# Sums of weights beside bank reads: fw2's first sums in pieces of 256 columns, three of fw1's sums one stage sooner, ScalarE first in block 1's products

## The chip, the cores and the metric

The kernel runs on one core of a Trainium2 chip. A core has five engines with a queue each: TensorE (PE in the profile; its weight loads are the row PEld), VectorE (DVE), ScalarE (ACT), GpSimd (POOL) and SyncE (SP, which here only issues DMAs). Each engine works through its queue in the order in which it was written, and waits on semaphores of the others. The metric is device time in microseconds for one launch, the median of several runs.

## The reference

One transformer-like block on x of 2 x 2048 tokens by 512 features, all in fp32, with six modulation rows from a condition:

```python
emb = silu(t) @ ada_w + ada_b
shift_msa, scale_msa, gate_msa, shift_mlp, scale_mlp, gate_mlp = split(emb, 6)
norm = ln(x) * (1 + scale_msa) + shift_msa
h = gelu(norm @ ssm_w1 + ssm_b1)                  # 512 -> 512
x = x + gate_msa * (h @ ssm_w2 + ssm_b2)          # 512 -> 512
norm2 = ln(x) * (1 + scale_mlp) + shift_mlp
hf = gelu_tanh(norm2 @ ff_w1 + ff_b1)             # 512 -> 1024
x = x + gate_mlp * (hf @ ff_w2 + ff_b2)           # 1024 -> 512
```

## The kernel before

The 4096 tokens are eight blocks of 512, four per batch element. Each block passes four products: hA (with w1), oA (with w2), hC (with fw1) and oC (with fw2). They are staggered: while PE works on hC and oC of block i, the other engines prepare the normalized and transposed input (nT) of later blocks.

To save matmuls, every product of two matrices is done in quarters by a scheme of seven products in place of eight (P1 to P7, Strassen-Winograd). Its price is sums of quarters on both sides. Four sums are needed for a side: two of them go in place or into a new tile first, the other two follow. `sums_of_first` and `sums_of_second` write them, and `cut_sum` (L311) issues them, whole or in pieces along the second axis. Sums of weights are done once (fw2's again for the second batch element), sums of activations (nS, hSA, hSC) for every block. PE's own order of the seven is P1, P2, P6, P5, P7, P3, P4. They accumulate in PSUM banks with the tags y, x, y, v, y, v, y, so a bank must be read out before a later product adds to it. `group` (L391) issues them; after each one a reader on DVE or ACT takes the bank. For hA and hC these are L565 or L563 (first use), L571, L578 and L581 on DVE and activations on ACT (L572, L579, L582, L585), for oA and oC L613 on DVE.

Block 0's hC is done so, in two groups. From block 1 on hC is one list of 26 products (`products`, L712), of sums of 4 x 4 quarters of fw1 with sums of 4 x 2 quarters of the activations, which stand in place of 32. For this fw1's 16 quarters and 12 further places are turned into 28 registers by 37 sums (`HK_A`, in pieces of 256 columns, L650, or L648 where the sum is negated), all on DVE. They are taken off a list in order: `take(n)` gives the next n to the hooks of a stage. The activations' side (`HK_B`, 20 sums, L650) runs on POOL. A product's bank is read into one or two of eight destinations: a destination's first read is a copy with a sign on ACT (L726), later ones are adds on DVE (L729). Where one bank has readers of both kinds, they are ordered: the second waits for the first.

```python
for turn in (fresh_reads, other_reads)[:: 1 if last else -1]:
```

decides which goes first; `last` is true for block 7 only.

Nothing is scheduled automatically: each engine's order is the order in which the program is written. Helpers take `hooks`, lists of small operations that are called after a given product, and so land at that place in their engine's queue.

Around the change the stages are, by PE's time in the profile: oA_1 (to 72 us), hC_0 group 0 (to 85), hC_0 group 1 (85 to 98.6), hA_2 (98.6 to 110.7), oC_0 (110.7 to 134.9), block 1's products (134.9 to 159.3), oA_2. In hC_0 group 1 POOL has, at P6, fw2's first two sums (`fold5(8, 10)`), then the sums of nT of block 2 (nS, L311), fw2's third sum, and the sums of hC's output (hSC). fw2's fourth sum and the 20 sums of `HK_B` follow in hA_2 and oC_0. In the same stages DVE has the sums of fw1: two in hC_0 group 1, eight and then four at the end in hA_2, eighteen in oC_0, the last five in the products. It also reads the banks, turns nT of block 1 (L476) and takes statistics (L425, L426) of block 3. fw1's upper right part is loaded again (L933, 512 KB) in hC_0 group 1, since the first scheme's sums have overwritten it.

Of the kernel before, what the change touches and what calls it, by code (L numbers as in the profile page):

```python
# [38 lines left out]
ALU = mybir.AluOpType  # L39
# [101 lines left out]
def kernel(  # L141
# [16 lines left out]
    nc = tc.nc  # L158
# [148 lines left out]
    def cut_sum(eng, out, a, b, f, cut):  # L307

        n = out.shape[1] // cut
        for r in [slice(c * n, (c + 1) * n) for c in range(cut)]:  # L310
            eng.tensor_tensor(out[:, r], a[:, r], b[:, r], f)  # L311
# [7 lines left out]
            lambda: cut_sum(eng, s[2], q["12"], s[0], ALU.subtract, cut),  # L319
        ]  # L320

    def sums_of_second(q, s, eng, last_cut=1):

        return [
            lambda: cut_sum(eng, s[1], q["22"], q["12"], ALU.subtract, 1),
            lambda: cut_sum(eng, q["12"], q["12"], q["11"], ALU.subtract, 1),
            lambda: cut_sum(eng, s[0], q["22"], q["12"], ALU.subtract, last_cut),
            lambda: cut_sum(eng, s[2], q["21"], s[0], ALU.subtract, last_cut),
        ]

    def first_operands(q, s):
# [2 lines left out]
    def second_operands(q, s):  # L334
        return {"P1": q["11"], "P2": q["21"], "P3": q["22"], "P4": s[2], "P5": q["12"], "P6": s[0], "P7": s[1]}

    def thirds(t):
        return [t[:, j] for j in range(3)]
# [12 lines left out]
        for n, w in (("w2", w2), ("fw2", fw2))  # L351
    ]

    def weight_of_second(w_sb, s, gt, engs, last_cut=1):

        K = w_sb.shape[1]

        def fold(k):
            engs[k % len(engs)].tensor_tensor(w_sb[:, k, :], w_sb[:, k, :], gt, ALU.mult)

        ops = [lambda k=k: fold(k) for k in range(K)]
        lo, hi = w_sb[:, : K // 2, :], w_sb[:, K // 2 :, :]
        q = {
            "11": lo[:, :, : D // 2],
            "12": lo[:, :, D // 2 :],
            "21": hi[:, :, : D // 2],
            "22": hi[:, :, D // 2 :],
        }
        s = thirds(s)
        return second_operands(q, s), ops + sums_of_second(q, s, nc.gpsimd, last_cut)  # L370

    Q = P // C
    ORDER = ("P1", "P2", "P6", "P5", "P7", "P3", "P4")
# [32 lines left out]
    def hook(hooks, places, ops):  # L406

        for n, op in enumerate(ops):
            hooks.setdefault(places[min(n, len(places) - 1)], []).append(op)


    class Norm:
# [117 lines left out]
        def summed(self, eng):  # L530

            s = thirds(sums.tile([P, 3, C, KD // 2, HT // C], F32, tag="s", name=f"nS{self.name}"))
            h = self.nT.rearrange("p a (k h r) -> p a k h r", k=KD, h=2)
            lo, hi = h[:, :, : KD // 2], h[:, :, KD // 2 :]
            q = {
                "11": lo[:, :, :, 0],
                "12": lo[:, :, :, 1],
                "21": hi[:, :, :, 0],
                "22": hi[:, :, :, 1],
            }  # L540
            self.ops = second_operands(q, s)
            return sums_of_second(q, s, eng)
# [99 lines left out]
    def sums_of_registers(program, reg, engs):  # L642


        def op(n, d, f, a, b):
            eng = engs[n % len(engs)]
            if f == "n":
                nc.vector.scalar_tensor_tensor(reg[d], reg[a], -1.0, reg[b], ALU.mult, ALU.subtract)  # L648
            else:
                eng.tensor_tensor(reg[d], reg[a], reg[b], ALU.add if f == "+" else ALU.subtract)  # L650

        return [lambda z=(n,) + step: op(*z) for n, step in enumerate(program)]
# [19 lines left out]
    class Second:  # L672
# [6 lines left out]
        def group(self, g, rhs, hooks):  # L679
            hidden(f"hC_{self.i}_{g}", rhs, fw1_ops, fb1T, AF.Gelu_apprx_tanh, self.lo, self.hi, g, hooks)  # L680

        def products(self, fa, fb, hooks, last=False):


            ends = {b: n for n, (b, *_) in enumerate(HK_P)}
            starts = [(n, b) for n, (b, fresh, *_) in enumerate(HK_P) if fresh]
            stops = set(ends.values())
            for n, b in starts:
                stops |= {max([m for m in range(n) if HK_P[m][0] == b], default=ends[b])}
            ps = {  # L690
                b: ps_g.tile([P, 2, HT], F32, tag=tag, name=f"p{tag}_hC_{self.i}_{b}")
                for b, tag in HK_BANK.items()
            }
            left = [sum(d == r for (*_, rs) in HK_P for r, _ in rs) for d in range(8)]
            fresh_dest, done = set(range(8)), []

            def dest(d):
                f, col = d // 2, d % 2
                h = (self.lo, self.hi)[f // 2]
                return h[:, 2 * (f % 2) : 2 * (f % 2) + 2, col * HT : (col + 1) * HT]  # L700

            def activate():
                for d in done:
                    for j in range(2):
                        h = dest(d)[:, j]
                        m = 2 * (d // 2) + j
                        nc.scalar.activation(h, h, AF.Gelu_apprx_tanh, bias=fb1T[:, m : m + 1])  # L707
                done.clear()

            for n, (b, fresh, ra, rb, reads) in enumerate(HK_P):  # L710
                for j in range(2):
                    nc.tensor.matmul(  # L712
                        ps[b][:, j, :],
                        fa[ra][:, j * P : (j + 1) * P],
                        fb[rb].rearrange("p a (c q) -> p c a q", q=Q),
                        start=(fresh and j == 0),
                        stop=(n in stops),
                        skip_group_check=True,
                    )
                fresh_reads = [r for r in reads if r[0] in fresh_dest]  # L720
                other_reads = [r for r in reads if r not in fresh_reads]
                fresh_dest -= {d for d, _ in fresh_reads}
                for turn in (fresh_reads, other_reads)[:: 1 if last else -1]:
                    for d, sign in turn:
                        if turn is fresh_reads:
                            nc.scalar.activation(dest(d), ps[b], AF.Identity, scale=float(sign))  # L726
                        else:
                            op = ALU.add if sign > 0 else ALU.subtract
                            nc.vector.tensor_tensor(dest(d), dest(d), ps[b], op)  # L729
                activate()  # L730
                for d, _ in reads:
                    left[d] -= 1
                    if not left[d]:
                        done.append(d)
                for op in hooks.get(n, ()):
                    op()
            activate()
# [87 lines left out]
    def ssm_gate():  # L825
        make_gate(2, 0)
        found["w2"] = weight_of_second(w2_sb, w2_s, gate[2, 0], (nc.vector,))
# [7 lines left out]
    hooks = {}  # L835
# [12 lines left out]
    hooks = {}  # L848
# [12 lines left out]
    def ff_gate():  # L861
        make_gate(5, 0)
        found["fw2"] = weight_of_second(fw2_sb, fw2_s, gate[5, 0], (nc.vector,), 4)

    def fold5(lo, hi):
        return [lambda k=k: found["fw2"][1][k]() for k in range(lo, hi)]

    def gb5_0():
# [5 lines left out]
    hooks = {}  # L874
# [20 lines left out]
    hooks = {}  # L895
# [13 lines left out]
    hC = Second(0)  # L909
    n2[1] = Norm(1, 2)  # L910
    hooks = {}
# [8 lines left out]
    fa = [fw1_sb[:, k, f * 2 * P : (f + 1) * 2 * P] for f in range(4) for k in range(KD)] + [  # L920
        fw1_s[:, s, k, c * 2 * P : (c + 1) * 2 * P] for s in range(3) for k in range(2) for c in range(2)
    ]
    fb, fa_sums = {}, sums_of_registers(HK_A, fa, (nc.vector,))

    def take(n):
        ops = fa_sums[:n]
        del fa_sums[:n]
        return ops
# [8 lines left out]
    hooks = {}  # L937
# [10 lines left out]
    hooks = {}  # L948
    hook(hooks, ("P1",), hC.summed(1, nc.gpsimd, 2))
    hook(hooks, ("P4",), n2[1].moved() + fold5(11, 12))  # L950
    hook(hooks, ("P1", "P2", "P6", "P6", "P5", "P5", "P7", "P3"), take(8))
    hA[2] = First(2, n1[2].ops, hooks, on_act=True)
    run(take(4))
    n1[3] = Norm(3, 1)
    hooks = {}
# [11 lines left out]
    for i in range(1, NBLK):  # L967
        nxt, nx2, last = i + 1 < NBLK, i + 2 < NBLK, i + 1 == NBLK
        hC = Second(i)
        hooks = {}  # L970
# [11 lines left out]
        if fold:  # L982
            hook(hooks, (2, 6, 23, 25), fold[:4])
        hook(hooks, (20,), hC.summed(0, nc.gpsimd))
        hC.products(fa, fb[i], hooks, last)

        hooks = {}
        hook(hooks, EARLY, hC.summed(1, nc.gpsimd if nxt else nc.vector))
# [15 lines left out]
        hooks = {}  # L1004
# [54 lines left out]
        if refold5:  # L1059
            load_w("fw2", fw2, fw2_sb)  # L1060
            make_gate(5, b)
            fw2_ops, fold = weight_of_second(fw2_sb, fw2_s, gate[5, b], (nc.vector,))
        hooks = {}
# [52 lines left out]
```

## Time and profile before

| | us |
|---|---|
| median of 3 runs | 603.66 |
| lowest, highest | 603.02, 604.52 |
| the profiled execution | 603.54 |
| its span, first to last instruction | 601.7 |
| PE busy in the span | 592.5 (98%) |
| DVE, ACT, POOL busy | 376.1, 218.7, 397.1 |
| granted TensorE clock | 0.999 |

The profile shows one execution. A row of a timeline gives the start, the duration, the engine, the line, the operation, what it writes and reads, the tile's size and the count, and in brackets how long the engine was idle before it and what released it. A row of the waits view gives the engine and tile that waited, the one waited for, the total in us, how often, and the longest. Busy time of PE is modelled from its instructions, so starts are the better measure.

### The profile page before, as it was taken

Reading aid. Unit: us, or ns where it says so; the run is one execution under the profiler, and the core shown is the slowest. Engines: PE = TensorE matmul, PEld = TensorE weight load, DVE = VectorE, ACT = ScalarE, POOL = GpSimd, SP = SyncE. Lnnn points to the kernel's source line nnn. Section 1 sums busy time; section 2 is a strip of 40 time slices with the busy share of each in tenths; the row PEclk is TensorE's granted clock in tenths of the full one; section 3 lists DMA queues with packets and bytes.
Section 4 is the critical chain, followed back from the end, with each engine's and each line's share of the span. In section 5 each row is a group of like instructions: output and inputs, shape, how many; then the busy total and the mean of one; then the engine's idle time right before and its main releaser. Section 6 shows DMA issues by size and latency. Waiting matters only on the chain.

```text
span 601.7 us, 8144 instructions
## 1 busy us (share of the span) xinstructions
PE 592.5 (98%) x2827; PEld 509.8 (85%) x2827; DVE 376.1 (63%) x638; ACT 218.7 (36%) x363; POOL 397.1 (66%) x459
## 2 busy tenths in 40 slices
PE   8999999999999999999999999999999999999997
PEld 4787887887888888888888888888888888888886
DVE  5978988997754475645754458644565336467642
ACT  3234247304532254323731346123553225212420
POOL 2878688998735896549978398885983695540110
PEclk9999999999999999999999999999999999999999
DMA  8980222300223003340051611321020300022001
GB/s 323 413 349 14 58 71 70 106 35 36 52 89 105 36 2 87 141 139 1 5 140 52 202 42 28 113 70 71 1 58 14 105 36 0 2 54 88 1 0 70
DMA packets 23116, 49.31 MB, mean 82 GB/s; under 512 B 4340, under 2 KB 4896, under 8 KB 22180
## 3 DMA queue, kind: packets, MB, share of 16 engines
q1 hardware_dynamic: 20032, 44.58, 22.3%
q10 hardware_dynamic: 3044, 4.23, 2.7%
q8 instruction: 22, 0.36, 0.2%
q14 instruction: 18, 0.15, 0.1%
HBM read 25.72 MB, written 8.39 MB: 57 GB/s over the span
## 4 chain that ended last, share of the span: by engine, by line
PE 92%; DVE 2%; DMA 2%; POOL 1%; issue 1%; ACT 1%; ACTq 1%; SPq 0%; DVEq 0%
PE py_oC L391 18%; PE px_hC L712 10%; PE pv_oC L391 9%; PE py_hA L391 9%; PE py_oA L391 8%; PE pv_hC L712 8%; PE py_hC L712 8%; PE px_oC L391 5%; PE pv_hA L391 4%; PE pv_oA L391 4%; PE px_hA L391 2%; PE px_oA L391 2%; DMA ada<-in_L_cond_ada_w_dram 2%; PE py_hC L391 1%; PE pv_hC L391 1%
## 5 line engine op out<-in xcount | busy, mean ns | idle before, releaser
L625 POOL TENSOR_TENSOR x<-x,gb 128x512 f32<-128x512 f32 x64 | 79.8, 1279 | 9.4 <-DVE gb L869 3.5
L508 ACT ACTIVATE nT<-nT,mod,mod 128x512 f32<-128x512 f32 x54 | 39.6, 802 | 103.1 <-DMA nT<-blocks 103.1
L311 POOL TENSOR_TENSOR hSC<-hClo 128x512 f32<-128x512 f32 (+1 forms) x34 | 39.6, 1169 | 45.9 <-ACT hClo L707 37.8
L465 ACT ACTIVATE nT<-x,nmr,rstd 128x512 f32<-128x512 f32 x56 | 42.5, 803 | 58.7 <-POOL nmr L452 42.8
L434 POOL TENSOR_SCALAR ve<-mv 128x4 f32<-128x4 f32 x16 | 3.7, 231 | 86.6 <-DVE mv L426 86.4
L391 PE MATMUL py_oC<-fw_s,hSC 128*128 128x256 f32 x256 | 57.9, 379 | 0.0
L391 PEld LDWEIGHTS py_oC<-fw_s,hSC 128*128 128x128 f32 x256 | 48.6, 190 | 6.6
L613 DVE TENSOR_TENSOR x<-py_oC,x 128x512 f32<-128x512 f32 (+1 forms) x36 | 22.5, 628 | 40.7 <-PE py_oC L391 40.7
L425 DVE BATCH_NORM_STATS2 st<-x 128x6 f32<-128x512 f32 x64 | 43.4, 678 | 5.1 <-DMA x<-in_x_dram 4.8
L712 PE MATMUL py_hC<-forms,fw 128*128 128x256 f32 x168 | 40.8, 379 | 0.0
L476 DVE STREAM_TRANSPOSE blocks<-nT 128x512 f32<-128x512 f32 x56 | 37.7, 693 | 3.9 <-ACT nT L465 3.4
L729 DVE TENSOR_TENSOR hClo<-hClo,py_hC 128x512 f32<-128x512 f32 x42 | 28.5, 681 | 17.1 <-ACT hClo L726 9.4
L650 POOL TENSOR_TENSOR forms<-forms 128x256 f32<-128x256 f32 x48 | 35.4, 738 | 2.8
L712 PEld LDWEIGHTS py_hC<-forms,fw 128*128 128x128 f32 x168 | 31.9, 190 | 4.3
L613 DVE TENSOR_TENSOR x<-py_oA,x 128x512 f32<-128x512 f32 x32 | 22.0, 689 | 19.6 <-PE py_oA L391 19.0
L729 DVE TENSOR_TENSOR hChi<-hChi,pv_hC 128x512 f32<-128x512 f32 x35 | 23.3, 683 | 17.1 <-PE pv_hC L712 17.1
L391 PE MATMUL py_oA<-w_s,hSA 128*128 128x256 f32 x128 | 30.4, 381 | 0.2 <-DVE x L613 0.2
L391 PE MATMUL py_hA<-nS,w_s 128*128 128x256 f32 x128 | 30.4, 381 | 0.0
L707 ACT ACTIVATE hClo<-hClo,colsT 128x256 f32<-128x256 f32 x56 | 25.3, 500 | 11.5 <-DVE hClo L729 11.4
L391 PE MATMUL py_oC<-fw,hClo 128*128 128x256 f32 x128 | 28.9, 379 | 0.0
L391 PE MATMUL pv_oC<-fw,hClo 128*128 128x256 f32 x128 | 28.9, 379 | 0.0
L391 PE MATMUL py_oC<-fw_s,hChi 128*128 128x256 f32 x128 | 28.9, 379 | 0.0
(210 smaller groups left out, 1406.2 us busy)
## 6 DMA issues: line engine op xcount, KB each, us to landing
nT<-blocks SPq DMA_DIRECT2D x168, 64.0 KB, 2.0
out_dram<-x SPq DMA_DIRECT2D x15, 512.0 KB, 3.0
x<-in_x_dram SPq DMA_DIRECT2D x7, 1024.0 KB, 7.1
ada<-in_L_cond_ada_w_dram SPq DMA_DIRECT2D x6, 1024.0 KB, 9.5
fw<-in_L_cond_ff_w_dram SPq DMA_DIRECT2D x3, 2048.0 KB, 9.1
nT<-blocks ACTq DMA_DIRECT2D x56, 64.0 KB, 2.0
w<-in_L_cond_ssm_w_dram SPq DMA_DIRECT2D x3, 1024.0 KB, 7.4
x<-in_x_dram SPq DMA_DIRECT2D x2, 512.0 KB, 5.1
```

The costliest lines, as they stand in the source:

```text
L311: eng.tensor_tensor(out[:, r], a[:, r], b[:, r], f)
L391: nc.tensor.matmul(ps[b][j * apart][:, j, :], lhs(p, j, k), rhs(p, j, k), start=(fresh and j * (not apart) == 0 and k == 0), stop=(p in (" ...
L425: nc.vector.bn_stats(st, xs[self.i][:, c, :])
L465: nc.scalar.activation(t, x_c, AF.Identity, bias=self.nmr[:, c : c + 1], scale=self.rstd[:, c : c + 1])
L476: nc.vector.transpose(self.bl[:, :, :, c, :].rearrange("p m k q -> p k m q"), self.nT[:, c, :].rearrange("p (k m q) -> p k m q", k=KD, m=C),)
L508: nc.scalar.activation(dst, src, AF.Identity, bias=shift, scale=scale)
L613: nc.vector.tensor_tensor(d, ps[BANK[p]][:, js], d, ALU.add)
L625: lambda c=c: nc.gpsimd.tensor_tensor(xs[i][:, c, :], xs[i][:, c, :], gb, ALU.add)
L650: eng.tensor_tensor(reg[d], reg[a], reg[b], ALU.add if f == "+" else ALU.subtract)
L707: nc.scalar.activation(h, h, AF.Gelu_apprx_tanh, bias=fb1T[:, m : m + 1])
L712: nc.tensor.matmul(ps[b][:, j, :], fa[ra][:, j * P : (j + 1) * P], fb[rb].rearrange("p a (c q) -> p c a q", q=Q), start=(fresh and j == 0) ...
L729: nc.vector.tensor_tensor(dest(d), dest(d), ps[b], op)
```

## The change

There are three edits. fw2's first two sums are cut as its last two already were: with `cut` = 4 each is four instructions of 128 x 256 instead of one of 128 x 1024. The sums of nT and of fw2 for the second batch element, which use the same function, stay whole. In hA_2's stage eleven of fw1's sums are taken instead of eight; two of the three more stand at P1 and one at P2, and every later sum of fw1 moves up by three places in the list, so that two and not five are left for block 1's products. In block 1, as in block 7, ACT's first reads of a bank stand ahead of DVE's.

```diff
-    def sums_of_second(q, s, eng, last_cut=1):
+    def sums_of_second(q, s, eng, cut=1):
 
         return [
-            lambda: cut_sum(eng, s[1], q["22"], q["12"], ALU.subtract, 1),
-            lambda: cut_sum(eng, q["12"], q["12"], q["11"], ALU.subtract, 1),
-            lambda: cut_sum(eng, s[0], q["22"], q["12"], ALU.subtract, last_cut),
-            lambda: cut_sum(eng, s[2], q["21"], s[0], ALU.subtract, last_cut),
+            lambda: cut_sum(eng, s[1], q["22"], q["12"], ALU.subtract, cut),
+            lambda: cut_sum(eng, q["12"], q["12"], q["11"], ALU.subtract, cut),
+            lambda: cut_sum(eng, s[0], q["22"], q["12"], ALU.subtract, cut),
+            lambda: cut_sum(eng, s[2], q["21"], s[0], ALU.subtract, cut),
         ]
...
-        def products(self, fa, fb, hooks, last=False):
+        def products(self, fa, fb, hooks, act_first=False):
...
-                for turn in (fresh_reads, other_reads)[:: 1 if last else -1]:
+                for turn in (fresh_reads, other_reads)[:: 1 if act_first else -1]:
...
-    hook(hooks, ("P1", "P2", "P6", "P6", "P5", "P5", "P7", "P3"), take(8))
+    hook(hooks, ("P1",) * 3 + ("P2", "P2", "P6", "P6", "P5", "P5", "P7", "P3"), take(11))
     hA[2] = First(2, n1[2].ops, hooks, on_act=True)
     run(take(4))
...
-        hC.products(fa, fb[i], hooks, last)
+        hC.products(fa, fb[i], hooks, last or i == 1)
```

`weight_of_second` passes its argument on under the new name; `ff_gate` gives 4 for fw2 before and after.

On PE, ACT and SP the same instructions stand in the same order. On POOL two become eight at one place. On DVE the count is the same: between the reads of hA_2 the sums stand 3, 6, 1, 1 (after P1, P2 to P5, P7, P3) where they stood 1, 5, 1, 1, and ahead of the products' reads of banks 3, 2 and 5 (the first four DVE reads) two sums are left.

More of the change, by code (lines that the diff above doesn't have):

```diff
@@ L352, with weight_of_second @@
     ]
-    def weight_of_second(w_sb, s, gt, engs, last_cut=1):
+    def weight_of_second(w_sb, s, gt, engs, cut=1):
         K = w_sb.shape[1]
@@ L369, in weight_of_second @@
         s = thirds(s)
-        return second_operands(q, s), ops + sums_of_second(q, s, nc.gpsimd, last_cut)
+        return second_operands(q, s), ops + sums_of_second(q, s, nc.gpsimd, cut)
     Q = P // C
```

## The prediction

> **What bounds the kernel now.** I read the page's head first, then TensorE's waits, then the timelines around the two longest.
>
> ```profile
> span 601.7 us, 8144 instructions
> PE 592.5 (98%) x2827; PEld 509.8 (85%) x2827; DVE 376.1 (63%) x638; ACT 218.7 (36%) x363; POOL 397.1 (66%) x459
> ...
> PE 92%; DVE 2%; DMA 2%; POOL 1%; issue 1%; ACT 1%; ACTq 1%; SPq 0%; DVEq 0%
> ```
>
> TensorE (PE) sets the end: 98% busy, 92% of the chain. The change touches no matmul, so it can only win the time in which PE waits. The waits view says where that is:
>
> ```profile
> PE px_hC L712 <- DVE hChi L729: 1.0, 1, 1.0
> PE pv_hC L391 <- DVE hChi L565: 0.5, 1, 0.5
> PE py_hC L391 <- POOL nS L311: 0.5, 1, 0.5
> PE px_hC L712 <- ACT hClo L726: 0.3, 1, 0.3
> ```
>
> The third lies at 76 us, ahead of all that is changed. In PE's timeline the last wait is at 143.57 us: from 160 us to the end no matmul waits, so what PE gains before then should reach the end.
>
> **Stall A**, in hC_0's second group (PE, then DVE, then POOL):
>
> ```profile
> 90.50 1.89 PE L391 MATMUL pv_hC<-nT,fw 128*128 128x256 f32 x8
> 92.56 1.99 PE L391 MATMUL py_hC<-nS,fw_s 128*128 128x256 f32 x8 [0.17 <-DVE hClo L565]
> 95.06 1.99 PE L391 MATMUL pv_hC<-nT,fw_s 128*128 128x256 f32 x8 [0.51 <-DVE hChi L565]
> 96.89 1.89 PE L391 MATMUL py_hC<-nS,fw 128*128 128x256 f32 x8
> ```
> ```profile
> 89.59 2.32 DVE L650 TENSOR_TENSOR fw<-fw 128x256 f32<-128x256 f32 x1
> ...
> 92.43 1.98 DVE L650 TENSOR_TENSOR fw<-fw 128x256 f32<-128x256 f32 x1
> ```
> ```profile
> 89.20 2.42 POOL L311 TENSOR_TENSOR fw_s<-fw 128x1024 f32<-128x1024 f32 x1
> 91.70 2.42 POOL L311 TENSOR_TENSOR fw<-fw 128x1024 f32<-128x1024 f32 x1
> ```
>
> Undisturbed groups of eight start 1.727 us apart. From 90.50 to 96.89 is 6.39 us for three, 5.18 undisturbed: A costs 1.21 us, more than the 0.68 shown as waits, since a pipeline restarts too. The cause: two 256-column sums of fw1 on DVE (VectorE), 0.42 us each at best (from 546 us on, with POOL, which is GpSimd, idle), take 2.32 and 1.98. Each ends just after a 1024-column sum of fw2 on POOL, and the bank reads at L565 stand behind them.
>
> **Stall B**, in block 1's 26 products (PE, DVE, ACT):
>
> ```profile
> 140.06 1.03 PE L712 MATMUL py_hC<-forms,fw 128*128 128x256 f32 x4
> 141.42 1.13 PE L712 MATMUL px_hC<-forms,fw_s 128*128 128x256 f32 x4 [0.34 <-ACT hClo L726]
> 143.57 1.13 PE L712 MATMUL px_hC<-forms,fw_s 128*128 128x256 f32 x4 [1.01 <-DVE hChi L729]
> ```
> ```profile
> 140.00 0.68 DVE L729 TENSOR_TENSOR hChi<-hChi,px_hC 128x512 f32<-128x512 f32 x1
> 140.60 0.42 DVE L648 SCALAR_TENSOR_TENSOR fw<-fw_s,fw 128x256 f32<-128x256 f32 x1
> 141.40 0.69 DVE L729 TENSOR_TENSOR hClo<-hClo,py_hC 128x512 f32<-128x512 f32 x1 [0.39 <-ACT hClo L726]
> 142.01 0.91 DVE L650 TENSOR_TENSOR fw<-fw 128x256 f32<-128x256 f32 x1
> 142.84 0.68 DVE L729 TENSOR_TENSOR hChi<-hChi,px_hC 128x512 f32<-128x512 f32 x1
> ```
> ```profile
> 140.77 0.60 ACT L726 ACTIVATE hClo<-px_hC 128x512 f32<-128x512 f32 x1 [2.51 <-POOL rstd L450]
> ```
>
> The products start at 134.88 and the next stage at 159.25: 24.37 us. Block 2 does the same 26 in 22.48 (207.77 to 230.25 along the chain), 26 x 0.863 = 22.45. B costs 1.9 us. Number the products from 0. ACT's (ScalarE's) read of product 3's bank starts only after DVE's ends (140.0 to 140.6); product 7 refills that bank and waits. DVE's read of product 4 then waits for ACT's result, an fw1 sum (142.01) comes next, and the read of product 5 starts at 142.84; product 8 needs it. Five sums of fw1 are interleaved with these reads.
>
> [...] 2.32 and 1.98 us beside 1024-column POOL sums, 0.83 to 0.97 beside 256-column ones, while L729, whose second input is a PSUM bank, keeps 0.68. [...] The trace has 2.42 us for 1024 columns and 0.72 for 256, or 2.2 ns a column with some 0.15 us fixed[...].
>
> **Part 1: fw2's first two sums in four pieces each.** Two POOL instructions of 2.42 become eight. The same shape in the rows of 100.96 and 117.11 takes 3.03 to 3.36 for four, so 6.1 to 6.7 for eight against 4.9: 1.2 to 1.8 more on POOL. POOL next sat idle 1.50 us before nS at 95.62, which waits for ACT's nT (L508, done 95.54). So nS starts 0 to 0.3 late; each further DVE sum beside POOL's holds it up by some 0.2 (0.91 against 0.72). Its third sum ends at 99.6 and hA_2's P6 wants it at 102.07 - 1.21 = 100.86, so this costs nothing. Later on POOL: hSC_1's first s0 piece (about 114.7; P6 of oC_0 wants it at 118.04 - 1.21 = 116.8) and block 1's forms (all wanted more than 5 us after they are made) keep over 1 us too. The DVE sums should drop to 0.83-0.97: L565 for P6 then follows its matmuls at 90.7, the second sum ends near 92.2, and L565 for P5 starts at 92.4, its matmuls' end, and is done at 93.1; P3 wants the bank at 93.96. **Gain 1.21**, bounds 0.9 to 1.21 (PE cannot gain more here).
>
> **Part 2: three fw1 sums earlier.** The order of hA_2's stage becomes: three sums (not one) ahead of DVE's L571 (px_hA), six (not five) between it and L578 (py_hA), one more before L581. DVE sat idle 2.50 us before L571 and 0.66 before L578, so most of it is covered. But the first three fall beside POOL's 1.27 us nS sums, so each may wait out one; L571 (PE 1.21 earlier: due 101.1) can be 0.65 late. Six sums at 0.78 to 0.87 then take 4.7 to 5.2, L578 ends between 107.2 and 108.1, and P4 of hA_2 wants its bank at 108.98 - 1.21 = 107.77. **Cost 0 to 0.5, taken 0.2.** The third sum also waits for the reloaded fw1 quarter (issued 92.43, 3.7 us to land): long there. Behind L581 the DVE queue runs about 0.5 late, and catches up in oC_0, where it idled 0.23 to 0.63 before each of four reads. SP and ACT issue the same DMAs in the same order.
>
> **Parts 2 and 3 at stall B.** Three of the five sums leave the products, and two stay ahead of product 3's read. With ACT first, ACT reads product 3 from about 138.6, and DVE's reads of 3, 4 and 5 follow each other. In the frame of before: two reads of product 1 to 139.2, one sum to 139.6, then reads to 140.2, 140.8, 141.4; product 7 wants the first at 140.92 and product 8 the third at 141.79. **Gain 1.9.** Against it: PE is now about 1.0 earlier, while POOL's forms end where they did or up to 0.9 later (137 to 137.7), so the sum that took 0.41 at 137.7 now meets POOL: +0.45 on DVE, which uses up the margin at product 8. **Cost 0 to 0.5, taken 0.2.** The later reversals (products 13 and 15) make DVE wait for ACT, behind ACT's 0.8 us normalizations (L465): DVE's reads of 13 and 14 would end about 151.2 in before's frame, product 17 starts at 151.44, so nothing.
>
> **Sum.** 1.21 + 1.9 - 0.2 - 0.2 = 2.7. The profiled execution took 603.54 with a span of 601.7: about 599.0 and 600.8 after. The median of the runs is 603.66, 0.12 above it: 603.66 - 2.7 = **600.9**. With the bounds of 1.8 (0.9 + 1.9 - 0.5 - 0.5) to 3.1 and a median's scatter of 0.3 the case reaches from 600.2 to 602.2. About 0.3%, or 1.8 us, is what a measurement of this kernel can tell from no change; that line is at 601.85.
>
> **Rivals.**
> - The wait moves (0.20): six sums push P4 of hA_2 late by its full 0.5, and DVE reaches the products so late that half of B stays (0.95). Gain 1.21 + 0.95 - 0.5 = 1.7: 602.0, just above the line. For it: the contended rows; against it: the idle time in hA_2 and oC_0.
> - The lock is not what stretches the two sums (0.05): A stays, B goes less the 0.2 for P4: 603.66 - 1.7 = 602.0. For it: one place only shows 2 us; against it: both ends match POOL's.
> - Slower (0.04): pieces under contention price POOL out. It decides at hA_2's P6: slack 1.26 + idle 1.50. Eight pieces of p cost PE 8p - 4.9 - 2.76; at p = 1.35 that eats the whole 3.1, and at 1.58, 1.8 more: 605.5. Against it: pieces beside DVE sums show at most 0.91.
> - It does what it says (0.71): 600.9.
>
> The first two straddle the line: a third of them goes to faster, and of the likeliest case a twentieth to no change. Faster 0.76, same 0.20, slower 0.04. Range 600.1 to 602.3: below the likeliest by scatter, above to hold the two middle rivals.
>
> **What would show it.** Right: the two L650 rows near 90 and 92 us under 1 us, L311 as eight rows of 0.7 to 0.9, no wait at L565; products within 22.5 to 23 us; the oA_2 stage at about 156.6. Part 2 wrong: a PE wait for hA L578 near 108. Part 3 wrong: PE still waiting for L729 at product 7 or 8. The whole wrong: a new PE wait after 160 us, or on POOL near 101 or 117.

## Result and profile after

The changed kernel takes 600.51 us (median of 5 runs, 600.44 to 600.91); the kernel before took 603.12 in the same comparison (5 runs, 602.97 to 604.52). The ratio is 0.9953, 95% interval 0.9939 to 0.9968: faster by about 2.6 us. The profiled execution took 600.48, span 598.7, which is 3.0 us below that of before. The forecast was 600.9, and 2.7 us less than before.

The page's head of the changed kernel, and its chain by engine:

```profile
span 598.7 us, 8148 instructions
PE 591.4 (99%) x2827; PEld 510.1 (85%) x2827; DVE 374.3 (63%) x638; ACT 218.8 (37%) x363; POOL 399.1 (67%) x465
...
PE 94%; DMA 2%; POOL 1%; DVE 1%; ACTq 1%; ACT 1%; issue 0%; SPq 0%
```

PE issues the same 2827 matmuls; its share goes up from 98 to 99% as its waits went. All the waits of PE that are left in the waits view:

```profile
PE pada L261 <- DMA ada<-in_L_cond_ada_w_dram: 1.5, 2, 1.3
PE idle L774 <- POOL ident masks.py:199: 1.3, 1, 1.3
PE py_hC L391 <- POOL nS L311: 0.5, 1, 0.5
PE py_oA L391 <- DVE x L613: 0.2, 1, 0.2
PE pv_oA L391 <- DVE x L613: 0.2, 1, 0.2
```

The waits for L565, L726 and L729 are gone and no other came. These five were there before, ahead of all that is changed.

**Stall A.** PE's timeline of the changed kernel in hC_0's second group, then DVE's, then POOL's:

```profile
90.56 1.89 PE L391 MATMUL pv_hC<-nT,fw 128*128 128x256 f32 x8
92.29 1.89 PE L391 MATMUL py_hC<-nS,fw_s 128*128 128x256 f32 x8
94.02 1.89 PE L391 MATMUL pv_hC<-nT,fw_s 128*128 128x256 f32 x8
95.75 1.89 PE L391 MATMUL py_hC<-nS,fw 128*128 128x256 f32 x8
```
```profile
89.65 0.66 DVE L650 TENSOR_TENSOR fw<-fw 128x256 f32<-128x256 f32 x1
90.77 0.69 DVE L565 TENSOR_TENSOR hClo<-py_hC,colsT 128x512 f32<-128x512 f32 x1 [0.46 <-PE py_hC L391]
91.38 0.51 DVE L650 TENSOR_TENSOR fw<-fw 128x256 f32<-128x256 f32 x1
92.49 0.69 DVE L565 TENSOR_TENSOR hChi<-pv_hC,colsT 128x512 f32<-128x512 f32 x1 [0.61 <-PE pv_hC L391]
```
```profile
89.28 3.20 POOL L311 TENSOR_TENSOR fw_s<-fw 128x256 f32<-128x256 f32 x4
92.45 2.79 POOL L311 TENSOR_TENSOR fw<-fw 128x256 f32<-128x256 f32 x4
95.70 1.27 POOL L311 TENSOR_TENSOR nS<-nT 128x512 f32<-128x512 f32 x1 [0.47 <-ACT nT L508]
```

The two sums of fw1 fell from 2.32 and 1.98 us to 0.66 and 0.51. DVE now waits for PE ahead of both L565, where PE waited for DVE; the groups follow every 1.727 us. Of POOL's 1.50 us idle before nS 0.47 is left, and nS starts at 95.70 as against 95.62.

**Stall B.** DVE, ACT and PE in block 1's products:

```profile
136.28 0.39 DVE L648 SCALAR_TENSOR_TENSOR fw<-fw_s,fw 128x256 f32<-128x256 f32 x1
136.59 1.28 DVE L729 TENSOR_TENSOR hChi<-hChi,pv_hC 128x512 f32<-128x512 f32 x2
137.78 0.45 DVE L650 TENSOR_TENSOR fw<-fw 128x256 f32<-128x256 f32 x1
138.16 0.67 DVE L729 TENSOR_TENSOR hChi<-hChi,px_hC 128x512 f32<-128x512 f32 x1
138.76 0.67 DVE L729 TENSOR_TENSOR hClo<-hClo,py_hC 128x512 f32<-128x512 f32 x1
139.35 0.67 DVE L729 TENSOR_TENSOR hChi<-hChi,px_hC 128x512 f32<-128x512 f32 x1
```
```profile
137.45 0.60 ACT L726 ACTIVATE hClo<-px_hC 128x512 f32<-128x512 f32 x1 [0.33 <-PE px_hC L712]
```
```profile
139.78 1.89 PE L712 MATMUL px_hC<-forms,fw_s 128*128 128x256 f32 x8
```

Only two sums stand among the reads, ACT takes product 3's bank 3.3 us earlier than before (140.77; the products start 1.15 earlier), and DVE's last read shown ends at 140.0. Product 8 is the second half of PE's row of eight and starts at about 140.64: a margin of 0.6 us where there was a wait of 1.0. The products take 156.19 - 133.73 = 22.46 us, which is 26 times the undisturbed 0.863: no time is lost among them.

### The profile page after: what moved, and what is told of

It is laid out like the page before. It is cut to its first block, busy times and chain, and to the rows that moved or that the text cites. A ratio compares the mean times of both kernels' runs of the same rounds, so it can differ in the third digit from the quotient of the medians.

```text
span 598.7 us, 8148 instructions
## 1 busy us (share of the span) xinstructions
PE 591.4 (99%) x2827; PEld 510.1 (85%) x2827; DVE 374.3 (63%) x638; ACT 218.8 (37%) x363; POOL 399.1 (67%) x465
## 4 chain that ended last, share of the span: by engine, by line
PE 94%; DMA 2%; POOL 1%; DVE 1%; ACTq 1%; ACT 1%; issue 0%; SPq 0%
PE py_oC L391 18%; PE px_hC L712 10%; PE pv_oC L391 9%; PE py_hA L391 9%; PE py_oA L391 8%; PE py_hC L712 8%; PE pv_hC L712 8%; PE px_oC L391 5%; PE pv_hA L391 4%; PE pv_oA L391 4%; PE px_hA L391 2%; PE py_hC L391 2%; PE px_oA L391 2%; DMA ada<-in_L_cond_ada_w_dram 2%; PE pv_hC L391 1%; PE pt L494 1%
## 5 line engine op out<-in xcount | busy, mean ns | idle before, releaser
L311 POOL TENSOR_TENSOR hSC<-hClo 128x512 f32<-128x512 f32 (+1 forms) x34 | 40.1, 1183 | 42.9 <-ACT hClo L707 38.7
L613 DVE TENSOR_TENSOR x<-py_oC,x 128x512 f32<-128x512 f32 (+1 forms) x36 | 22.5, 629 | 40.4 <-PE py_oC L391 40.3
L729 DVE TENSOR_TENSOR hClo<-hClo,py_hC 128x512 f32<-128x512 f32 x42 | 28.4, 681 | 16.6 <-ACT hClo L726 10.4
L650 POOL TENSOR_TENSOR forms<-forms 128x256 f32<-128x256 f32 x48 | 35.5, 740 | 2.8
L613 DVE TENSOR_TENSOR x<-py_oA,x 128x512 f32<-128x512 f32 x32 | 22.0, 689 | 19.5 <-PE py_oA L391 19.0
L729 DVE TENSOR_TENSOR hChi<-hChi,pv_hC 128x512 f32<-128x512 f32 x35 | 23.4, 684 | 17.1 <-PE pv_hC L712 17.1
L391 PE MATMUL pv_oC<-fw,hSC 128*128 128x256 f32 x128 | 28.9, 379 | 0.0
```

The source lines that it names most:

```text
L391: nc.tensor.matmul(ps[b][j * apart][:, j, :], lhs(p, j, k), rhs(p, j, k), start=(fresh and j * (not apart) == 0 and k == 0), stop=(p in (" ...
L613: nc.vector.tensor_tensor(d, ps[BANK[p]][:, js], d, ALU.add)
```

## Experiments

Two differences of PE's start times say for each run where it gained: from oA_1 to hA_2 (stall A lies in it) and from the products to oA_2 (stall B). The last column has PE's waits among the products.

| kernel | time, median (runs) | oA_1 to hA_2 | products | waits there |
|---|---|---|---|---|
| before | 603.12 to 603.83 by comparison | 39.17 | 24.37 | 0.34, 1.01 |
| before, again | 603.48 (1) | 39.19 | 24.35 | 0.33, 1.00 |
| edit 1, pieces | 603.23 (20) | 37.97 | 26.32 | 0.60, 1.01 |
| edit 1, again | 602.53 (1) | 37.95 | 24.60 | 0.58, 1.01 |
| edit 2, sooner | 602.32 (20) | 39.21 | 22.96 | 0.19 |
| edit 3, order | 603.19 (12) | 39.18 | 23.75 | 1.03 |
| edits 2 and 3 | 601.76 (6) | 39.21 | 22.46 | none |
| edits 1 and 2 | 600.87 (4) | 37.95 | 22.81 | none over 0.1 |
| edits 1 and 3 | 602.62 (12) | 37.96 | 24.58 | 1.69 |
| fw1's two sums moved | 601.48 (5) | 37.96 | 23.45 | 0.53 |
| pieces of 512 | 600.43 (4) | 37.96 | 22.45 | none |
| all three (after) | 600.51 (5) | 37.97 | 22.46 | none |
| last experiment | 601.97 (9) | 38.96 | 22.45 | none |

The medians of the kernel before differ by 0.7 us from comparison to comparison, so small differences between kernels of different comparisons are read from the starts.

My theory: A is DVE's sums of fw1 waiting for the end of POOL's sums of fw2 (in the kernel before they end at 91.91 and 94.41 us, each 0.29 after one of POOL's), worth 1.2; the prediction calls this the lock, the experiments the exclusion. B is the sums and the late ACT read together, worth 1.9; so they add. The rival: other waits set the time, and one of the edits does nothing or only moves a wait.

**Each edit alone, and edits 2 and 3.**

```diff
 edit 1
-            lambda: cut_sum(eng, s[1], q["22"], q["12"], ALU.subtract, 1),
-            lambda: cut_sum(eng, q["12"], q["12"], q["11"], ALU.subtract, 1),
+            lambda: cut_sum(eng, s[1], q["22"], q["12"], ALU.subtract, last_cut),
+            lambda: cut_sum(eng, q["12"], q["12"], q["11"], ALU.subtract, last_cut),
 edit 2
-    hook(hooks, ("P1", "P2", "P6", "P6", "P5", "P5", "P7", "P3"), take(8))
+    hook(hooks, ("P1",) * 3 + ("P2", "P2", "P6", "P6", "P5", "P5", "P7", "P3"), take(11))
 edit 3
-        hC.products(fa, fb[i], hooks, last)
+        hC.products(fa, fb[i], hooks, last or i == 1)
```

Edit 1 alone:

> Before with the first edit alone: fw2's first two sums in four pieces each. Exclusion theory (DVE's sums of fw1 wait out a whole POOL sum of fw2): the two L650 rows in hC_0's second group fall from 2.3 and 2.0 us to under 1, the group loses no time, hA_2 starts 1.1 to 1.2 us sooner; block 1's products still stall by 1.9 us or a little more (24.4 to 24.8 us from first product to oA_2). 1.0 to 1.3 us faster in all. Rival (something else holds DVE there, the pieces only cost POOL 1.3 us more): hA_2 starts where it did, and the time stays or grows by up to 1 us.

Edit 2 alone:

> Before with the second edit alone: eleven sums of fw1 in hA_2's stage instead of eight. Queue theory (stall B is sums of fw1 standing between the bank reads on DVE): most of B goes. ACT's read of product 3 still follows DVE's, so products 7 and 8 wait some 0.1 and 0.5 us: products take 22.8 to 23.2 us instead of 24.4, and the whole is 1.2 to 1.6 us faster. Rival (the order of the two readers is what makes B): products stay at 24 us or more, under 0.5 us faster. Either way stall A stays (1.2 us), and hA_2's P4 shows no wait, since PE comes 1.2 us later there than in the changed kernel.

Edit 3 alone:

> Before with the third edit alone: ScalarE's first reads of a bank ahead of VectorE's in block 1. Queue theory: DVE still has four sums of fw1 among the first five reads, the read of product 5 ends near 143.1 instead of 143.5, product 8 still waits 1 us or more; products take 23.7 to 24.1 us, 0.3 to 0.7 us faster. Rival (the order of the readers makes B): products fall to 22.5 to 22.8 us, 1.6 to 1.9 us faster.

Edits 2 and 3:

> Before with the second and third edits, without the pieces. Queue theory: B goes wholly (products 22.5 to 22.6 us), A stays at 1.2 us: 1.8 to 2.0 us faster. If the pieces are also needed for B (through POOL or through the time at which PE arrives), products stay above 23 us.

Measured, with ratios to the kernel before (603.43 here): edit 1 alone 1.0003 (0.9990 to 1.0017), edit 2 0.9986 (0.9979 to 0.9992), edit 3 0.9991 (0.9983 to 1.0000), edits 2 and 3 0.9971 (0.9959 to 0.9982). By the medians edit 2, edit 3 and the two together gave 1.11, 0.24 and 1.67 us, each about 0.1 below the range expected.

Edit 1 alone missed. Its profile has A's 1.2 us (37.97 as against 39.17), and yet no gain in the median. PE's timeline in the products of edit 1 alone:

```profile
140.52 1.13 PE L712 MATMUL px_hC<-forms,fw_s 128*128 128x256 f32 x4 [0.60 <-ACT hClo L726]
142.66 1.57 PE L712 MATMUL px_hC<-forms,fw_s 128*128 128x256 f32 x4 [1.01 <-DVE hChi L729]
144.02 1.91 PE L712 MATMUL pv_hC<-forms,fw_s 128*128 128x256 f32 x4
```

The first wait is 0.26 longer than before's. PE arrives 1.2 us earlier, but DVE's reads of products 3 to 5 come only 0.9 earlier: five sums of fw1 stand among the reads as before, and the first of them now meets POOL's forms and takes 0.93 us instead of 0.39.

```profile
136.25 0.93 DVE L650 TENSOR_TENSOR fw<-fw,fw_s 128x256 f32<-128x256 f32 x1
```

Besides, the rows from the second wait on take 1.57 and 1.91 us, where four matmuls take 1.03, or 1.13 after a wait. What that is, a run further below shows.

Edits 2 and 3 do not touch A (39.2 in all three). On B edit 2 alone is worth 1.4, edit 3 alone 0.6, and together 1.9. Edit 3 alone leaves product 8 waiting 1.03 us, since with the reads earlier the last sum of fw1 falls into a POOL sum of hA of 512 columns (hSA, L311). POOL and DVE in edit 3 alone:

```profile
140.88 1.27 POOL L311 TENSOR_TENSOR hSA<-hA 128x512 f32<-128x512 f32 x1
```
```profile
141.05 1.38 DVE L650 TENSOR_TENSOR fw<-fw 128x256 f32<-128x256 f32 x1
142.36 0.67 DVE L729 TENSOR_TENSOR hChi<-hChi,px_hC 128x512 f32<-128x512 f32 x1
```

**Edit 1 with one of the others.**

Edits 1 and 2:

> The changed kernel with the third edit undone (VectorE first in block 1 as before). Queue theory: A gone; in the products ACT reads product 3 after DVE, product 7 waits about 0.1 and product 8 up to 0.5 us: 0 to 0.6 us slower than the changed kernel, that is 2.0 to 2.6 us faster than before in the median of that pair. If the order is the larger part of B, it is 1 us or more slower than the changed kernel.

Edits 1 and 3:

> The changed kernel with the second edit undone (eight sums in hA_2's stage, five left for the products). Queue theory: A gone, B nearly whole: products 23.7 to 24.5 us, 1.3 to 1.9 us slower than the changed kernel, so 1.2 to 1.8 us faster than before. Rival (order alone removes B): within 0.3 us of the changed kernel.

Measured (before 603.83 here): edits 1 and 2 0.9954 (0.9940 to 0.9969), edits 1 and 3 0.9982 (0.9971 to 0.9993). Without the order of reads 0.35 us of B is left (22.81). Without the earlier sums all of B is left and more: the last sum takes 1.37 us beside hSA, and product 8 waits 1.69. So without edit 2 a part of A's gain is given back in the products: 0.2 us against the kernel before (24.58 and 24.37), 0.8 against edit 3 alone (23.75). Edit 3 is the smallest of the three once edit 2 is there.

**The exclusion, tested by moving DVE's side.** fw2's sums stay whole on POOL, and fw1's two sums go to the front of hA_2's stage; nothing else is changed from the kernel before.

```diff
-    hook(hooks, ("P2", "P6"), take(2))
...
-    hook(hooks, ("P1", "P2", "P6", "P6", "P5", "P5", "P7", "P3"), take(8))
+    hook(hooks, ("P1", "P1", "P1", "P2", "P6", "P6", "P5", "P5", "P7", "P3"), take(10))
```

> Before, with fw2's first two sums left whole (2 x 1024 columns), and the two sums of fw1 that stood beside them on VectorE moved to the front of hA_2's stage. Exclusion theory: with no VectorE instruction of two SBUF inputs beside the whole sums, stall A goes although POOL is unchanged: hC_0's second group loses nothing, hA_2 starts 1.1 to 1.2 us sooner, and hA_2's P1 takes three sums at up to 1.4 us each without a PE wait; the products keep stall B: 1.0 to 1.3 us faster. Rival (POOL's long sums hold up something else, such as the bank reads themselves or ACT): the L565 rows stay late and A stays.

Measured: 601.48, 0.9967 (0.9954 to 0.9980), more than expected. POOL and DVE in this kernel:

```profile
89.17 2.44 POOL L311 TENSOR_TENSOR fw_s<-fw 128x1024 f32<-128x1024 f32 x1
91.68 2.37 POOL L311 TENSOR_TENSOR fw<-fw 128x1024 f32<-128x1024 f32 x1
```
```profile
90.66 0.69 DVE L565 TENSOR_TENSOR hClo<-py_hC,colsT 128x512 f32<-128x512 f32 x1 [1.03 <-PE py_hC L391]
92.39 0.69 DVE L565 TENSOR_TENSOR hChi<-pv_hC,colsT 128x512 f32<-128x512 f32 x1 [1.04 <-PE pv_hC L391]
...
140.32 0.42 DVE L650 TENSOR_TENSOR fw<-fw 128x256 f32<-128x256 f32 x1
```

With whole POOL sums A is gone all the same (37.96), and L565, which reads PSUM and a small tile, keeps 0.69 us beside a POOL sum of 1024 columns. So it was not POOL's length as such, but sums on DVE that end with POOL's while bank reads stand behind them. The stretched L650 rows, which have both inputs in SBUF, end 0.28 to 0.29 us after a POOL sum: at 91.91 and 94.41 in the kernel before (POOL at 91.62 and 94.12), at 142.43 in edit 3 alone (142.15). The surplus came in the products (23.45; 24.60 in the second execution of edit 1 alone), where two of the five sums of fw1 no longer meet a POOL sum: the first takes 0.39 us, not 0.92, and the last 0.42, not 0.90, since POOL reaches hSA later (at 141.08; at 140.45 in the first execution of edit 1 alone, where the last sum took 0.90 too).

**The length of the pieces.** The changed kernel with pieces of 512 columns for these two sums. Against the kernel before, with edits 2 and 3 left out here:

```diff
-            lambda: cut_sum(eng, s[1], q["22"], q["12"], ALU.subtract, 1),
-            lambda: cut_sum(eng, q["12"], q["12"], q["11"], ALU.subtract, 1),
+            lambda: cut_sum(eng, s[1], q["22"], q["12"], ALU.subtract, min(last_cut, 2)),
+            lambda: cut_sum(eng, q["12"], q["12"], q["11"], ALU.subtract, min(last_cut, 2)),
```

> The changed kernel with fw2's first two sums in two pieces of 512 columns instead of four of 256. Exclusion theory: a sum of fw1 waits out at most one piece of 1.27 us, so the two L650 rows show 0.9 to 1.6 us; the L565 reads come up to 0.7 us late, but their banks are wanted only 1.5 us after they are filled: no PE wait, the same time as the changed kernel within 0.2 us, with POOL 0.6 us less busy. If the size must be 256 for PE not to wait, 0.3 us or more slower than the changed kernel.

Measured: 600.43, 0.9948 (0.9933 to 0.9963): no different from the changed kernel. DVE's two sums, and POOL's four pieces:

```profile
89.72 1.20 DVE L650 TENSOR_TENSOR fw<-fw 128x256 f32<-128x256 f32 x1
...
91.45 0.93 DVE L650 TENSOR_TENSOR fw<-fw 128x256 f32<-128x256 f32 x1
```
```profile
89.36 2.74 POOL L311 TENSOR_TENSOR fw_s<-fw 128x512 f32<-128x512 f32 x2
92.03 2.72 POOL L311 TENSOR_TENSOR fw<-fw 128x512 f32<-128x512 f32 x2
```

The sums take nearly twice as long as beside pieces of 256, but the next L565 starts 0.1 us later at most, so PE doesn't see it. POOL spends 5.46 us on four pieces and 5.99 on eight.

**What edit 1 alone lost.** The same kernels once more, edit 1 alone and the kernel before:

> The pieces alone once more, for the size of the stall in block 1's 26 products and for the granted clock there. If what its first profile showed was a fixed consequence of the waits, the products take 26 us again with waits of 0.6 and 1.0 us at products 7 and 8 and a granted clock near 0.82 for some us behind them. If the clock's fall was chance, the products take 24.4 to 24.7 us (the waits alone, as with the pieces and the order of reads) with the clock at full through them, and the span is 1.5 us or more shorter.

> The kernel before once more, for how much its two stalls vary from one execution to the next. If they are set by the order of the queues, hA_2 starts 1.2 us late again (98.6 us) and the products take 24.2 to 24.5 us. If the times at which transfers and GpSimd's sums end vary, the start of hA_2 or the length of the products differs by 0.5 us or more from the first profile.

Measured: edit 1 alone 602.53, before 603.48. PE in this execution of edit 1 alone:

```profile
140.43 1.13 PE L712 MATMUL px_hC<-forms,fw_s 128*128 128x256 f32 x4 [0.58 <-ACT hClo L726]
142.57 1.13 PE L712 MATMUL px_hC<-forms,fw_s 128*128 128x256 f32 x4 [1.01 <-DVE hChi L729]
143.54 1.03 PE L712 MATMUL pv_hC<-forms,fw_s 128*128 128x256 f32 x4
```

The stretch from 140 to 145 us in the two executions of edit 1 alone, first and again (the stretch's length; busy time and instructions of PE, PEld, DVE, ACT and POOL; then PEclk, DMA share, GB/s):

```profile
140.00:145.00 5.00, 3.48 (x11) 2.60 (x12) 3.50 (x6) 2.36 (x4) 4.68 (x6) 0.82 0.00 0
```
```profile
140.00:145.00 5.00, 3.56 (x15) 2.85 (x16) 3.81 (x7) 2.80 (x5) 4.68 (x6) 1.00 0.00 0
```

The same waits, but in the first execution PE's mean granted clock is 0.82 from 140 to 145 us, 0.84 from 145 to 150, and 1.00 before and after. Its four matmuls at 144.02 are followed by the next row at 145.73, 1.71 us later; in the second execution the same step takes 0.86 (143.54 to 144.40). My estimate from these figures is one stretch at half the clock, 3.4 us long, from 143.2 to 146.6 us. The clock that is missing, 0.18 and 0.16 of 5 us each, comes to 1.7 us, and the products took 1.7 us longer. In the second execution the clock stayed at 1.00, the products took 24.60, and A's gain came through but for 0.2: 602.53 is 0.95 below the kernel before.

The mean granted clock of every run is on record, and it sorts the twenty runs of the first comparison. Eleven with 0.999 or more took 602.61 to 603.32, four with 0.997 took 604.28 to 604.53, and five with 0.994 took 605.78 to 606.74. A loss of 1.7 us is 0.003 of such a run, so by this estimate the second group fits one stretch at half the clock and the third fits two; where they lay is known for the profiled run alone. The eleven have a median of 602.76, which is 0.6 below the 603.33 of the 42 of 49 runs of the kernel before with such a clock. So edit 1 alone gave 0.6 by these medians and 0.95 by the two executions, not quite the 1.0 to 1.3 expected.

**The stalls that are left.** From the changed kernel, for L613 and nS: three gb5 operations later, the scales of block 2's norm cut between POOL and DVE, and block 2's biases in block 1's products. The two new functions, `scales_pool` and `scales_dve`, are left out here: they replace `scales` by two operations on POOL and four on DVE.

```diff
-    hook(hooks, ("P1",), hA_sums[2:3] + [gb5_0] + fw1_sums[3:] + gb5[:3])
+    hook(hooks, ("P1",), hA_sums[2:3] + [gb5_0] + fw1_sums[3:])
...
-    hook(hooks, ("P5",), n2_sums[:1] + [n1[2].scales])
-    hook(hooks, ("P7",), n2_sums[1:] + [lambda c=c: n1[2].normal(c) for c in range(C)] + gb5[3:])
+    hook(hooks, ("P5",), n2_sums[:1] + [n1[2].scales_pool])
+    hook(hooks, ("P7",), n2_sums[1:] + gb5)
+    hook(hooks, ("P3",), [n1[2].scales_dve] + [lambda c=c: n1[2].normal(c) for c in range(C)])
...
-    hook(hooks, ("P1",), biases(2, gb[2]))
...
+        if i == 1:
+            hook(hooks, (10, 11, 12, 13), biases(2, gb[2]))
```

> The changed kernel, with the two stalls of TensorE that its profile still shows (at 66.75 and 68.95 us for L613, and at 76.5 us for nS) attacked by earlier work on VectorE: the first three of the five gb5 operations go from oA_1's P1 to its P7, the scales of group 2's norm are cut in two (two operations on GpSimd at P5, four on VectorE at P3 with the normals), and the biases of group 2 go from P1 of hC_0's first group into block 1's products. If those waits come from what stands ahead of them in VectorE's and GpSimd's queues, the waits of 0.2, 0.2 and 0.5 us and the restarts after them go: 1.0 to 1.7 us less than the changed kernel, 598.8 to 599.5. If the work that is moved only meets other waits (the biases among the 26 products' bank reads, the scales late for hC_0), the time is 600.3 to 601.5 and a wait at L391 for n or nS, or one among the products, shows it.

Measured: 601.97 (9 runs, 601.41 to 604.35), 0.9980 (0.9967 to 0.9993), about 1.5 slower than the changed kernel (1.2 by its six runs with a granted clock of 1.0, whose median is 601.66). The waits for L613 and nS went and the products took 22.45 us, but a longer wait came. PE, then DVE:

```profile
79.21 1.97 PE L391 MATMUL py_hC<-nS,fw_s 128*128 128x256 f32 x8 [1.62 <-DVE hClo L584]
```
```profile
74.49 1.22 DVE L468 TENSOR_TENSOR e<-r,ve 128x4 f32<-128x4 f32 x1 [0.76 <-POOL r L460]
75.75 0.16 DVE L469 SCALAR_TENSOR_TENSOR e<-e,r 128x4 f32<-128x4 f32 x1
75.95 1.12 DVE L470 SCALAR_TENSOR_TENSOR rstd<-e,r 128x4 f32<-128x4 f32 x1
77.10 0.16 DVE L471 SCALAR_TENSOR_TENSOR nmr<-mv,rstd 128x4 f32<-128x4 f32 x1
```

(L584 is L565 of the other listings.) The four operations on 128 x 4 stand in DVE's queue ahead of a bank read; two of them take 0.16 us and two, beside POOL's sums of nT, 1.22 and 1.12 (they end at 75.71 and 77.07, POOL's sums at 75.70 and 77.05). From oA_1 to hA_2 is 38.96 us, 1.0 more than in the changed kernel. A miss, above both ranges expected: the change made the same kind of stall as A at a new place. The rest of this profile's delay, 2.2 us, lies at the start and is told in the last section.

## Why the prediction was right

The mechanism and both sizes held; the time came out 0.4 us under the forecast, within the range.

- **Stall A, 1.21:** measured 39.17 - 37.97 = 1.20. The sums came to 0.66 and 0.51, below the 0.83 to 0.97 that I took from contended rows, and L565 starts at 92.49, where 92.4 was worked out. The first of them takes 2.32, 1.20 and 0.66 us beside POOL sums of 1024, 512 and 256 columns, and A goes as well when the two are moved away from whole POOL sums. The rival in which the lock does not stretch them is ruled out by that. Of the 1.21 us 0.68 were waits. The other 0.53 is the restart, by the rows of before: twice 0.10 (eight matmuls take 1.99 us after a wait, 1.89 else) and twice the 0.16 by which undisturbed rows overlap (1.89 long, 1.727 apart).
- **POOL's pieces, 6.1 to 6.7 us:** 5.99. nS starts 0.08 later (0 to 0.3 was said) and its third sum ends at 99.74 (99.6). The rival in which POOL becomes the bound needed 1.35 us a piece; the pieces took 0.75.
- **Part 2 at hA_2's P4, 0.2 taken of 0 to 0.5:** 0. L571 starts at 101.35, about 0.2 late, not 0.65, although two of the three sums ahead of it took 1.37 and 1.38 us; the six sums take 4.72 us, the low end of 4.7 to 5.2; L578 ends at 107.3, and P4 starts at 107.83 with no wait. DVE in the changed kernel:

```profile
101.35 0.68 DVE L571 TENSOR_TENSOR hA<-px_hA,hA 128x512 f32<-128x512 f32 x1
...
106.67 0.68 DVE L578 TENSOR_TENSOR hA<-py_hA,hA 128x512 f32<-128x512 f32 x1
```

- **Stall B, 1.9:** 24.37 - 22.46 = 1.91. Edits 2 and 3 together give it without edit 1, edit 2 alone 1.4 and edit 3 alone 0.6.
- **The meeting with POOL at product 8, 0.2 taken of 0 to 0.5:** 0. POOL's forms end at 137.95, even later than the 137.7 I allowed, but the sum at 136.28 starts just ahead of a POOL form and is done in 0.39 us, and the one at 137.78 takes 0.45 as POOL ends. I had put 0.45 more on one of them. The step is right in kind: in edit 1 alone the sum that I named (0.39 us at 137.71 before; 0.41, which I wrote, is the next one's) does meet POOL's forms and takes 0.93. With three sums gone from the products it did not happen.
- **The sum:** 2.7 forecast, 3.06 in the profiles (3.11 of both stalls, less 0.05 of a later oA_1). The two costs of 0.2, which did not occur, are the terms that were mis-sized. The forecast time also stood on a median 0.12 above the profiled execution. The medians of the comparison differ by 2.61 only, which looks nearer to the forecast; but the profiled execution of the kernel before lies 0.42 above its median there, that of the changed kernel 0.03 below, so this nearness is luck. Why some runs of the kernel before are 0.5 us shorter than the profiled ones, no profile shows.

The prediction said that what PE gains before 160 us reaches the end; 3.06 us gained at oA_2 and 3.0 of the span agree. It was made for the three edits together and did not ask what each is worth alone. There they depend on each other: PE that comes 1.2 us earlier to reads that come only 0.9 earlier waits longer. The second execution of edit 1 alone has B grown by 0.2, and edits 1 and 3 have it 0.8 above edit 3 alone (24.58 and 23.75).

## What to carry to other kernels

When a small operation takes several times its usual time, look for the instruction on another engine at whose end it ends (0.29 us after it in stall A), and count what is queued behind it: the cure may be to cut the long one, or to move the short one to where nothing urgent stands behind it, and both gave the same 1.2 us here. Cut only as fine as the next deadline asks: pieces of 512 columns were as good as 256 here (600.43 and 600.51 us). After one wait goes, the same engine arrives earlier at the next one (PE by 1.2 us at the products), so a part of an edit's gain (0.2 to 0.8 of 1.2 us here) may show only together with the edit that clears the way further on.

## What the runs showed that I had not expected

The granted clock fell to half beside short waits of PE. In three of the thirteen profiled executions its mean over five microseconds drops: to 0.82 and 0.84 in edit 1 alone (140 to 150 us), to 0.66 in edit 2 alone (10 to 15), to 0.67 and 0.99 in the last experiment (10 to 20). Each time 1.7 us of clock are missing, which is 3.4 us at half the clock; the half is read from the rows in edit 1 alone and is an estimate for the other two, as are the times that follow. In edit 1 alone it fell at 143.2 us, half a microsecond after the second of two waits of 0.60 and 1.01 us. In edit 2 alone and the last experiment it fell at about 11.2 and 11.7 us, in or just after the second of two waits for ada, of 0.80 and 1.63 us and of 0.83 and 1.44, and the 32 matmuls behind it took 1.94 us instead of 1.08; oA_1 starts 1.4 and 2.2 us late, the waits included. The same pair of waits left the clock at 1.00 in the other execution of edit 1 alone, and 0.71 and 1.44 us at the start did so there too. What decides whether the clock falls, no run here shows.

So in the first execution of edit 1 alone 1.7 us were lost beyond the 1.61 us of the two waits. How often the clock fell, the runs with a mean granted clock below 0.999 tell: 9 of 20 of edit 1 alone, 1 of 12 of edits 1 and 3, 7 of 49 of the kernel before in the comparison with edit 1, none of 12 of edit 3 alone, whose one wait among the products is 1.03 us. The five kernels with no wait of 0.6 us or more among the products or in hC_0 (after, edits 1 and 2, edits 2 and 3, the moved sums, the pieces of 512) have none in 24, and lie within 0.5 us in 4 to 6 runs each. But edit 2 alone, which has no such wait either, has 3 in 20, and the last experiment, with one of 1.62 us in hC_0, 3 in 9; their profiles put the one fall that they show at the start. That fewer waits further on mean fewer falls is my estimate from these counts and not shown.
